# Placing side work by TensorE time: half of the next image's preparation moved, and a step put between an operation and its transposes

## The chip, the cores and the metric

The kernel runs on one core of a Trainium2 chip. The metric is the device time of one execution in microseconds; the kernel before takes 1912.11 us, the median of three runs. Five engines work side by side on the core, each through its own list of instructions: TensorE (PE, matmuls and transposes), VectorE (DVE), ScalarE (ACT), GpSimd (POOL) and SyncE (SP), which here issues the transfers.

## The reference

The input is four images of 32 channels by 128 x 128 points, in float32. Two layers follow each other.

```python
# layer 0: attention over the 4096 positions of an image
xs = x.reshape(B, C, h, R, w, R).transpose(0, 1, 3, 5, 2, 4).reshape(B, C*R*R, h, w)   # R = 2
q = xs.reshape(B, C*R*R, 4096)                       # 128 values of 4096 positions
energy = einsum('bci,bcj->bij', q, q)
energy = energy / (d[:, :, None] * d[:, None, :])
attn = softmax(energy, axis=-1)
out = gamma * einsum('bcj,bij->bci', q, attn) + xs
# layer 1: on 4096 tokens of 128 values per image as the kernel lays them out
t = t + attn_linear(layer_norm(t))     # K, Q, V with 8 heads, K^T V first, no softmax
t = t + moe(layer_norm(t))             # 8 experts, the best two of a softmax router
```

In the kernel an image of layer 0 is a matrix of 4096 positions by 128 values. Its scaled energies are symmetric, so the kernel computes only one half of them and uses each block twice. Layer 1 works on 32 groups of 128 tokens by 128 values. It uses that K^T V is a product with the Gram matrix of the normalised tokens, so that one Gram matrix of 128 x 128 stands for all tokens.

## The kernel before

**Layer 0, `attend(b)`.** The 4096 positions are cut into 8 chunks of 512, and a chunk into 4 blocks of 128. The outer loop runs over the chunk `i`, the inner over the chunks `jc` up to and including `i`, and then over the 4 blocks `j` of `jc`. One step is: a matmul of 512 columns for the energies (`pe`, L272), the exponential on ScalarE (`pr`, L274), and a matmul that adds this block to the output of chunk `i` (`po`, L240). For `jc < i`, VectorE also transposes the exponentials in squares of 32 (`F`, L281), 16 transfers put the squares into place (`G`, L295), and four matmuls (`pg`, L209) add the other half to the output of chunk `jc`, followed by a VectorE addition (`o`, L219). These four come `LAG` units later than the block they belong to, from the list `late`. The blocks on the diagonal are shorter, and need transposes of their own (`ptd`, L251). An image has 144 steps.

**The preparation, `prep(b, kc)`.** A quarter of an image (two chunks) is loaded (`xx`), turned on TensorE (`ptq`, L173), copied by VectorE into `qT` (L176), squared and summed (`sq`, `ss`, L184 and L185), sent to GpSimd for the power of minus one half (`rn`, L111), multiplied by it (`qs`, L192), turned again on TensorE (`ptn`, L195) and copied by ScalarE into `qn` (L197), which the energies read. It is a generator with 9 steps.

**Layer 1, `layer1(b, st, alone)`.** A generator of about 166 steps. Its first half divides the outputs of layer 0 by the sums (`pbd` transposes on TensorE, `df` on VectorE, the addition into `T` on GpSimd), takes row statistics (`bs`, then a power on GpSimd), normalises on ScalarE (`xn`, L366) and adds up the Gram matrix (`pgram`, L409). Its second half applies the attention (`pat`, L464), normalises again (`xg`, L366), turns the result (`ptf`, L483), routes (`route`), turns the gates (`ptg`, L552), and runs the eight experts (`py`, L566 and L573).

**What sets the order.** The generators are side work: the loop at the end of the kernel draws steps from them between the steps of `attend`, so that their small operations lie between large matmuls. Each stream has a first step, a last step and a count, and the position is the number of the attention step:

```python
        else:
            streams.append((work_left, BEGIN, 140, SIDE))
        if b + 1 < B:
            for kc, at in enumerate((96, 124, 131, 137)):
                streams.append((prep(b + 1, kc, states[b + 1]), at, at + 9, 9))
```

So layer 1 of image `b - 1` runs inside the attention of image `b`, from step 14 to step 140, and all four quarters of image `b + 1` are prepared in the last third of image `b`. Layer 1 of the last image runs alone at the end (`alone` is true). What the loop draws is a wish: when the program is built, the framework may still move an instruction on its engine when it judges that its operands come late, but on the chip each engine takes its list in order. Buffers come from pools: `qn` has 11 buffers (`npool`), `qT` 5, the PSUM tiles `pt` and `py` two each, `po` and `pg` one each.

Of the kernel before, what the change touches and what calls it, by code (L numbers as in the profile page):

```python
# [10 lines left out]
F32 = mybir.dt.float32  # L11
# [8 lines left out]
def kernel(  # L20
# [35 lines left out]
    nc = tc.nc  # L56
    P = 128
# [4 lines left out]
    NCH = N // CH  # L62
    NJ = CH // P
    HW2 = W // 2
    KT = 32
# [4 lines left out]
    const = ctx.enter_context(tc.tile_pool(name="const", bufs=1))  # L70
    xin = ctx.enter_context(tc.tile_pool(name="xin", bufs=2))
    qpool = ctx.enter_context(tc.tile_pool(name="qpool", bufs=5))
    npool = ctx.enter_context(tc.tile_pool(name="npool", bufs=11))
    big1 = ctx.enter_context(tc.tile_pool(name="big1", bufs=1))
    opool = ctx.enter_context(tc.tile_pool(name="opool", bufs=NCH + 2))
    ppool = ctx.enter_context(tc.tile_pool(name="ppool", bufs=6))
# [2 lines left out]
    work = ctx.enter_context(tc.tile_pool(name="work", bufs=2))  # L79
# [7 lines left out]
    def psum_t(name):  # L87
        return ps_t.tile([P, CH], F32, tag="pt", name=name)
# [14 lines left out]
    ebd = const.tile([P, 4, D], F32, tag="eb", name="ebd")  # L103
# [6 lines left out]
    def pow_neg_half(dst, src):  # L110
        nc.gpsimd.tensor_tensor(dst, src, neg_half.to_broadcast(list(src.shape)), ALU.pow)  # L111
# [37 lines left out]
    def tokens(ap, b):  # L149
        return ap[b].rearrange("c (s k r) w -> s r c k w", s=2, r=2)  # L150
# [9 lines left out]
    def prep(b, kc, st):  # L160

        xx = xin.tile([P, 8, HW2, 2], F32, tag="xx", name=f"xx_{b}_{kc}")
        load_tokens(xx.rearrange("p k w r -> p k (w r)"), b, 8 * kc, 8)
        qT = qpool.tile([P, 2, NJ, P], F32, tag="qT", name=f"qT_{b}_{kc}")
        st.setdefault("qT", {})[2 * kc] = qT[:, 0]
        st["qT"][2 * kc + 1] = qT[:, 1]
        yield
        for g in range(2):
            pt = psum_t(f"ptq_{b}_{kc}_{g}")
            for jj in range(2):  # L170
                for r2 in range(2):
                    k = 4 * g + 2 * jj
                    nc.tensor.transpose(  # L173
                        pt[:, ts(2 * jj + r2, P)], xx[:, k : k + 2, :, r2].rearrange("p k w -> p (k w)"), ident
                    )
            nc.vector.tensor_copy(  # L176
                qT[:, :, 2 * g : 2 * g + 2, :].rearrange("p s j (r c) -> p (j r) s c", c=64),
                pt.rearrange("p (m s c) -> p m s c", s=2, c=64),
            )
            yield  # L180
        ss = stat.tile([P, 2 * NJ], F32, tag="ss", name=f"ss_{b}_{kc}")
        for s in range(2):
            sq = work.tile([P, NJ, P], F32, tag="sq", name=f"sq_{b}_{kc}_{s}", bufs=1)
            nc.vector.tensor_tensor(sq, qT[:, s], qT[:, s], ALU.mult)  # L184
            nc.vector.tensor_reduce(ss[:, ts(s, NJ)], sq, AX.X, ALU.add)  # L185
            yield
        rn = stat.tile([P, 2 * NJ, 1], F32, tag="rn", name=f"rn_{b}_{kc}")
        pow_neg_half(rn[:, :, 0], ss)
        yield
        for s in range(2):  # L190
            qs = work.tile([P, NJ, P], F32, tag="qs", name=f"qs_{b}_{kc}_{s}", bufs=2)
            nc.vector.tensor_tensor(qs, qT[:, s], rn[:, ts(s, NJ)].to_broadcast([P, NJ, P]), ALU.mult)  # L192
            pt = psum_t(f"ptn_{b}_{kc}_{s}")
            for j in range(NJ):
                nc.tensor.transpose(pt[:, ts(j, P)], qs[:, j, :], ident)  # L195
            qn = npool.tile([P, CH], F32, tag="qn", name=f"qn_{b}_{2 * kc + s}")
            nc.scalar.activation(qn, pt, AF.Copy)  # L197
            st.setdefault("qn", {})[2 * kc + s] = qn
            yield

    late = []
    clock = [0]
# [110 lines left out]
    def layer1(b, st, alone):  # L313
# [166 lines left out]
        def expert_rows(g):  # L480
            pt = psum_s(f"ptf_{b}_{g}")
            for j in range(4):
                nc.tensor.transpose(pt[:, ts(j, P)], normed[g][:, j, :], ident)  # L483
            nc.scalar.activation(xn[:, ts(g, 4), :], pt.rearrange("p (j t) -> p j t", t=P), AF.Copy)
# [42 lines left out]
            yield  # L527

        for u in range(6):
            for g in (2 * u, 2 * u + 1):  # L530
                if u < 4 and not alone:
                    transpose_rows(g)
                    yield
            if 0 <= u - 1 < 4:
                la = yield from attention_rows(u - 1)
                yield from row_stats(f"f{b}", u - 1, rsf, nbf)
                yield
                router_rows(u - 1, la)
                yield
            for g in (2 * u - 4, 2 * u - 3):  # L540
                if 0 <= u - 2 < 4:
                    norm_rows(g)
                    expert_rows(g)
                    yield
            if u in (2, 4):
                yield from route(u // 2 - 1)


        dst = tokens(out, b)
        for g in range(KT // 4):  # L550
            pt = psum_s(f"ptg_{b}_{g}")
            nc.tensor.transpose(pt[:, :P], gate[:, 4 * g : 4 * g + 16, :].rearrange("p j e -> p (j e)"), ident)  # L552
            gT = work.tile([P, P], F32, tag="gT", name=f"gT_{b}_{g}", bufs=2)
            nc.vector.tensor_copy(gT, pt[:, :P])
            pb = psum_s(f"pbe_{b}_{g}")
            nc.tensor.matmul(pb, gT, ebd.rearrange("p j c -> p (j c)"), start=True, stop=True)  # L556
            acc = work.tile([P, 4, D], F32, tag="acc", name=f"acc_{b}_{g}", bufs=2)
            nc.vector.tensor_tensor(acc, T[:, ts(g, 4), :], pb.rearrange("p (j c) -> p j c", c=D), ALU.add)
            yield
            for jj in range(2):  # L560
                tmp = work.tile([P, 2, 4, D], F32, tag="wide", name=f"tmp_{b}_{g}_{jj}")
                for jk in range(2):
                    j = 2 * jj + jk
                    k = 4 * g + j
                    py = psum_y(f"py_{b}_{k}_0")
                    nc.tensor.matmul(py, xn[:, k, :], ew_sb[:, 0:4, :], start=True, stop=True)  # L566
                    for e in range(4):
                        nc.vector.scalar_tensor_tensor(  # L568
                            acc[:, j, :], py[:, ts(e, D)], gate[:, k, e : e + 1], acc[:, j, :], ALU.mult, ALU.add
                        )  # L570
                    yield
                    py = psum_y(f"py_{b}_{k}_1")
                    nc.tensor.matmul(py, xn[:, k, :], ew_sb[:, 4:8, :], start=True, stop=True)  # L573
                    for e in range(4):
                        nc.scalar.activation(  # L575
                            tmp[:, jk, e, :], py[:, ts(e, D)], AF.Copy, scale=gate[:, k, 4 + e : 5 + e]
                        )
                    yield
                nc.gpsimd.tensor_tensor(tmp[:, :, 0:2], tmp[:, :, 0:2], tmp[:, :, 2:4], ALU.add)  # L579
                nc.gpsimd.tensor_tensor(tmp[:, :, 0], tmp[:, :, 0], tmp[:, :, 1], ALU.add)  # L580
                rows = acc[:, 2 * jj : 2 * jj + 2, :]
                nc.gpsimd.tensor_tensor(rows, rows, tmp[:, :, 0], ALU.add)
            for s in range(2):
                for r1 in range(2):
                    p0 = s * 64 + r1 * 32
                    nc.sync.dma_start(dst[s, r1, :, ts(g, 4), :], acc[p0 : p0 + 32])


    states = [{} for _ in range(B)]
    STEPS = NJ * NCH * (NCH + 1) // 2  # L590
    LAST = STEPS - NJ * NCH
    SIDE = 166
    BEGIN = 14

    first = prep(0, 0, states[0])
    next(first)
    load_weights()
    for _ in first:
        pass

    for b in range(B):
        streams = []
        if b == 0:
            for kc, begin, end in ((1, 0, 8), (2, 10, 26), (3, 30, 60)):
                streams.append((prep(0, kc, states[0]), begin, end, 9))
            streams.append((setup_weights(), 60, 70, 3))
        else:
            p = states[b - 1]
            work_left = layer1(b - 1, p, False)
            streams.append((work_left, BEGIN, 140, SIDE))  # L610
        if b + 1 < B:
            for kc, at in enumerate((96, 124, 131, 137)):
                streams.append((prep(b + 1, kc, states[b + 1]), at, at + 9, 9))
        done = [0] * len(streams)
        for t, _ in enumerate(attend(b, states[b])):
            for n, (steps, begin, end, count) in enumerate(streams):
                while t >= begin and done[n] * (end - begin) < (t + 1 - begin) * count:
                    next(steps, None)
                    done[n] += 1
        for steps, *_ in streams:  # L620
            for _ in steps:
                pass
# [42 lines left out]
```

## Time and profile before

| | before |
|---|---|
| three runs, us | 1914.57, 1911.74, 1912.11 |
| span of the profiled execution, us | 1915.9 |
| TensorE busy, share of the span | 95% |
| VectorE, ScalarE, GpSimd busy | 47%, 51%, 15% |
| granted TensorE clock, mean | 0.978 |
| share of TensorE on the chain that ended last | 79% |

A profile of one execution has several views. The page gives the busy time of each engine and the granted TensorE clock by slice. The view of waits says who waited for whom, with the total, the number and the longest, in microseconds. The view of windows gives, for a stretch of time, its length, the busy time with the number of records, the granted clock, the share of the transfer engines and their rate. The timeline lists instructions in order of time, with the idle time before them in brackets. A name on the left of an arrow is written, the names on the right are read.

### The profile page before, as it was taken

How to read it: one execution, taken by the hardware profiler on the slowest of the kernel's cores; microseconds unless marked ns; L12 is line 12 of the kernel's file. 1: busy time of each engine (PE TensorE's matmuls, PEld its weight loads, DVE VectorE, ACT ScalarE, POOL GpSimd, SP SyncE). 2: the span in 40 equal slices, each digit the busy share in tenths (PEclk: the TensorE clock that was granted, in tenths of full speed). 3: DMA queues.
4: the chain of work that ended last, by engine and by line, in shares of the span. 5: the costliest groups of instructions: out<-in, count | busy, mean ns of one | idle time of the engine just before them, and what ended most of it. 6: DMA issues, size and time to landing. Idle time of an engine off the chain costs nothing.

```text
span 1915.9 us, 21142 instructions
## 1 busy us (share of the span) xinstructions
PE 1817.3 (95%) x5474; PEld 921.4 (48%) x5474; DVE 907.9 (47%) x2201; ACT 974.8 (51%) x3117; POOL 293.1 (15%) x279
## 2 busy tenths in 40 slices
PE   6999999988999999999999999999999999999588
PEld 4445444444554444445555444445555544444543
DVE  3333232435355454543555445453545544543676
ACT  2554445445456555444657555444465654554454
POOL 0000000003000222201200122210210022220336
PEclk9999999999999999999999999999999999999789
DMA  5333334322232232343232323233422233245001
GB/s 117 77 87 75 95 90 106 95 69 61 66 86 69 58 90 73 78 110 76 56 83 71 88 65 85 70 84 76 99 64 67 72 74 77 73 97 117 1 11 34
DMA packets 142247, 145.68 MB, mean 76 GB/s; under 512 B 32528, under 2 KB 84784, under 8 KB 142128
## 3 DMA queue, kind: packets, MB, share of 16 engines
q1 hardware_dynamic: 138496, 142.73, 31.0%
q10 hardware_dynamic: 3632, 1.60, 0.4%
q8 instruction: 45, 0.74, 0.2%
q14 instruction: 74, 0.61, 0.1%
HBM read 18.38 MB, written 8.39 MB: 14 GB/s over the span
## 4 chain that ended last, share of the span: by engine, by line
PE 79%; DVE 8%; SPq 4%; POOL 4%; ACT 2%; DMA 2%; issue 1%; ACTq 0%; DVEq 0%; POOLq 0%
PE po L240 22%; PE pe L272 19%; PE pg L209 17%; PE py L573 5%; PE py L566 5%; SPq L295 4%; PE pat L464 1%; PE pbe L556 1%; DVE F L281 1%; DVE df L383 1%; POOL rsa L111 1%; PE ptd L251 1%; PE ptn L195 1%; DVE bs_a L352 1%; PE pgram L409 1%
## 5 line engine op out<-in xcount | busy, mean ns | idle before, releaser
L274 ACT ACTIVATE pr<-pe 128x512 f32<-128x512 f32 (+1 forms) x576 | 323.7, 562 | 526.7 <-PE pe L272 523.3
L240 PE MATMUL po<-pr,qT 128*128 128x512 f32 (+3 forms) x1152 | 551.9, 561 | 9.3 <-ACT pr L274 7.6
L281 DVE STREAM_TRANSPOSE F<-pr 128x512 f32<-128x512 f32 x448 | 311.5, 705 | 387.0 <-ACT pr L274 349.1
L272 PE MATMUL pe<-qn,qn 128*128 128x512 f32 x896 | 459.4, 594 | 0.0
L209 PE MATMUL pg<-G,qT 128*128 128x512 f32 x896 | 443.8, 597 | 7.6 <-DVE o L219 7.4
L240 PEld LDWEIGHTS po<-pr,qT 128*128 128x128 f32 x1152 | 213.6, 191 | 239.9 <-issue 188.2
L214 ACT ACTIVATE junk<-G 128x512 bf16<-128x512 f32 x448 | 276.7, 625 | 2.6 <-DMA G<-F 2.1
L209 PEld LDWEIGHTS pg<-G,qT 128*128 128x128 f32 x896 | 167.9, 192 | 203.8 <-issue 184.3
L575 ACT ACTIVATE tmp<-py,gate 128x128 f32<-128x128 f32 x512 | 145.3, 371 | 179.1 <-PE py L573 168.7
L272 PEld LDWEIGHTS pe<-qn,qn 128*128 128x128 f32 x896 | 159.2, 191 | 145.5 <-issue 145.4
L568 DVE SCALAR_TENSOR_TENSOR acc<-py,gate,acc 128x128 f32<-128x128 f32 x512 | 175.1, 348 | 107.9 <-PE py L566 95.3
L219 DVE TENSOR_TENSOR o<-o,pg 128x512 f32<-128x512 f32 x112 | 76.6, 684 | 195.0 <-PE pg L209 193.9
L579 POOL TENSOR_TENSOR tmp<-tmp 128x512 f32<-128x512 f32 x64 | 81.4, 1272 | 511.4 <-ACT tmp L575 511.3
L573 PE MATMUL py<-ew_sb,xn 128*128 128x512 f32 x256 | 132.8, 605 | 3.8 <-ACT tmp L575 3.8
L566 PE MATMUL py<-ew_sb,xn 128*128 128x512 f32 x256 | 130.1, 595 | 0.0
L274 ACT ACTIVATION_READ_ACCUMULATOR pr<-pe 128x1 f32 x576 | 115.1, 200 | 0.0
L111 POOL TENSOR_TENSOR rn<-ss,neg_half 128x8 f32<-128x8 f32 x16 | 26.2, 1640 | 501.8 <-DVE ss L185 501.8
L272 PE MATMUL pe<-qn 128*128 128x512 f32 (+3 forms) x256 | 90.1, 442 | 0.0
L214 ACT ACTIVATION_READ_ACCUMULATOR junk<-G 128x1 f32 x448 | 88.5, 197 | 0.0
L573 PEld LDWEIGHTS py<-ew_sb,xn 128*128 128x128 f32 x256 | 48.7, 194 | 64.2 <-issue 53.0
L111 POOL TENSOR_TENSOR rsf<-dm_f,neg_half 128x8 f32<-128x8 f32 x16 | 26.3, 1642 | 339.7 <-DVE dm_f L361 339.7
L566 PEld LDWEIGHTS py<-ew_sb,xn 128*128 128x128 f32 x256 | 48.0, 191 | 58.3 <-issue 43.0
(121 smaller groups left out, 1441.3 us busy)
## 6 DMA issues: line engine op xcount, KB each, us to landing
G<-F SPq DMA_DIRECT2D x1792, 64.0 KB, 2.0
xx<-in_x_dram SPq DMA_DIRECT2D x64, 128.0 KB, 2.9
T<-in_x_dram SPq DMA_DIRECT2D x16, 512.0 KB, 7.2
out_dram<-acc SPq DMA_DIRECT2D x128, 64.0 KB, 1.8
ew_sb<-in_L_ffn_expert_w_dram ACTq DMA_DIRECT2D x1, 512.0 KB, 5.4
raw_w<-in_L_attn_Wv_dram ACTq DMA_DIRECT2D x1, 512.0 KB
raw_w<-in_L_attn_Wk_dram ACTq DMA_DIRECT2D x1, 256.0 KB
raw_w<-in_L_attn_Wq_dram ACTq DMA_DIRECT2D x1, 256.0 KB
```

The costliest lines, as they stand in the source:

```text
L209: nc.tensor.matmul(pg.rearrange("p (a f) -> p a f", a=4), st["qT"][i][:, ib, :], G[:, :, ib], start=(ib == 0), stop=(ib == NJ - 1),)
L214: nc.scalar.activation(junk, G[:, :, ib], AF.Copy, accum_out=st["sums"][:, NJ * i + ib, jc : jc + 1])
L240: nc.tensor.matmul(po[:, lo:hi], qT[blk // NJ][:, blk % NJ, :], w, start=(count[0] == 1), stop=(count[0] == total))
L272: nc.tensor.matmul(pe[:, c0:], qn[jc][:, ts(j, P)], qn[i][:, c0:], start=True, stop=True)
L274: nc.scalar.activation(pr[:, c0:], pe[:, c0:], AF.Exp, accum_out=sums[:, t, i : i + 1])
L281: nc.vector.transpose(Fb[:, :, :, j, :], pr)
L295: nc.sync.dma_start(G[ts(q, S), a].rearrange("p ib f -> p (ib f)"), F[ts(a, S), q].rearrange("p ib j c -> p (ib j c)"),)
L566: nc.tensor.matmul(py, xn[:, k, :], ew_sb[:, 0:4, :], start=True, stop=True)
L568: nc.vector.scalar_tensor_tensor(acc[:, j, :], py[:, ts(e, D)], gate[:, k, e : e + 1], acc[:, j, :], ALU.mult, ALU.add)
L573: nc.tensor.matmul(py, xn[:, k, :], ew_sb[:, 4:8, :], start=True, stop=True)
L575: nc.scalar.activation(tmp[:, jk, e, :], py[:, ts(e, D)], AF.Copy, scale=gate[:, k, 4 + e : 5 + e])
L579: nc.gpsimd.tensor_tensor(tmp[:, :, 0:2], tmp[:, :, 0:2], tmp[:, :, 2:4], ALU.add)
```

## The change

Four things change. The side work is placed by `clock`, which counts the TensorE work of the attention in units, as a percentage of the image's `UNITS`, and no longer by the number of the step; layer 1 gets 7% to 97%. Quarters 2 and 3 of the next image are prepared inside that image (2% to 20% and 30% to 50%), quarters 0 and 1 still in the image before (66% to 84% and 85% to 99%); the pool of `qn` then has 10 buffers. In `prep` the two multiplications become steps of their own, before the transposes that need them, and the count of steps is 10. In `layer1` the second half is reordered: the attention rows of a group come before the next group's `ptx` transposes, the `ptf` transposes of a group come one step after its normalisation, and the gates are turned ahead of the group that uses them. It is meant to give each chain of VectorE, GpSimd and ScalarE operations some TensorE work to hide behind.

```diff
-    npool = ctx.enter_context(tc.tile_pool(name="npool", bufs=11))
+    npool = ctx.enter_context(tc.tile_pool(name="npool", bufs=10))
...
+        scaled = []
         for s in range(2):
             qs = work.tile([P, NJ, P], F32, tag="qs", name=f"qs_{b}_{kc}_{s}", bufs=2)
             nc.vector.tensor_tensor(qs, qT[:, s], rn[:, ts(s, NJ)].to_broadcast([P, NJ, P]), ALU.mult)
+            scaled.append(qs)
+            yield
+        for s, qs in enumerate(scaled):
             pt = psum_t(f"ptn_{b}_{kc}_{s}")
...
         for u in range(6):
+            if 0 <= u - 1 < 4:
+                la = yield from attention_rows(u - 1)
             for g in (2 * u, 2 * u + 1):
                 if u < 4 and not alone:
                     transpose_rows(g)
                     yield
             if 0 <= u - 1 < 4:
-                la = yield from attention_rows(u - 1)
                 yield from row_stats(f"f{b}", u - 1, rsf, nbf)
...
             for g in (2 * u - 4, 2 * u - 3):
-                if 0 <= u - 2 < 4:
+                if 0 <= g - 1:
+                    expert_rows(g - 1)
+                    yield
+                if 0 <= g:
                     norm_rows(g)
-                    expert_rows(g)
                     yield
             if u in (2, 4):
                 yield from route(u // 2 - 1)
+        expert_rows(KT // 4 - 1)
+        yield
...
-        for g in range(KT // 4):
+        gates = {}
+
+        def transpose_gate(g):
             pt = psum_s(f"ptg_{b}_{g}")
...
+        transpose_gate(0)
+        yield
+        for g in range(KT // 4):
...
+                if jj == 0 and g + 1 < KT // 4:
+                    transpose_gate(g + 1)
...
-            streams.append((work_left, BEGIN, 140, SIDE))
+            streams.append((layer1(b - 1, states[b - 1], False), 7, 97, 161))
         if b + 1 < B:
-            for kc, at in enumerate((96, 124, 131, 137)):
-                streams.append((prep(b + 1, kc, states[b + 1]), at, at + 9, 9))
+            nxt = states[b + 1]
+            streams.append((prep(b + 1, 0, nxt), 66, 84, 10))
+            streams.append((prep(b + 1, 1, nxt), 85, 99, 10))
+            carried.append((prep(b + 1, 2, nxt), 2, 20, 10))
+            carried.append((prep(b + 1, 3, nxt), 30, 50, 10))
         done = [0] * len(streams)
-        for t, _ in enumerate(attend(b, states[b])):
+        start = clock[0]
+        for _ in attend(b, states[b]):
+            t = 100 * (clock[0] - start) / UNITS
             for n, (steps, begin, end, count) in enumerate(streams):
-                while t >= begin and done[n] * (end - begin) < (t + 1 - begin) * count:
+                while t >= begin and done[n] * (end - begin) < (t - begin) * count:
```

## The prediction

> **What bounds the kernel now.** I read the page first (engines, slices, clock), then the waits of TensorE, then windows cut at the stages, then a timeline of the longest wait.
>
> ```profile
> PE 1817.3 (95%) x5474; PEld 921.4 (48%) x5474; DVE 907.9 (47%) x2201; ACT 974.8 (51%) x3117; POOL 293.1 (15%) x279
> PE   6999999988999999999999999999999999999588
> PEclk9999999999999999999999999999999999999789
> ```
>
> TensorE is busy from slice 1 to slice 36; no other engine comes near. So the time is TensorE's work plus what TensorE loses. What it loses has names:
>
> ```profile
> PE ptn L195 <- DVE qs L192: 26.1, 8, 6.4
> ...
> PE po L240 <- ACT pr L274: 7.6, 6, 2.6
> ...
> PE pg L209 <- DVE o L219: 7.4, 6, 1.9
> PE ptf L483 <- ACT xg L366: 5.9, 6, 3.0
> ```
>
> The first line is the preparation: its second transposes wait for the scaled rows. Where these losses lie, the windows tell (time, busy, records, clock, transfer share, rate). I take as lost in a window its length minus busy times clock, so that a slow clock counts too.
>
> ```profile
> 341.00:364.00 23.00, 20.04 (x56) 0.93 0.32 80
> 364.00:386.00 22.00, 20.63 (x63) 1.00 0.43 108
> 386.00:408.00 22.00, 15.45 (x58) 0.84 0.33 79
> 440.00:490.00 50.00, 43.07 (x164) 0.97 0.28 70
> 550.00:796.00 246.00, 246.00 (x684) 1.00 0.31 76
> 796.00:816.00 20.00, 18.09 (x45) 0.91 0.31 76
> 837.00:866.00 29.00, 25.10 (x82) 0.88 0.43 105
> 899.00:930.00 31.00, 27.95 (x100) 0.94 0.35 81
> 1757.00:1810.00 53.00, 35.63 (x184) 0.81 0.22 43
> ```
>
> Between the stages nothing is lost (550 to 796: 246.00 of 246.00 at full clock). Lost are 22 - 15.45 x 0.84 = 9.0 us in 386 to 408, and in the same way 4.4, 1.4, 8.2, 3.5, 6.9 and 4.7 us in the other short ones. Images 2 and 3 repeat each other: the windows 1257:1277, 1298:1327 and 1360:1391 again lose 3.5, 6.9 and 4.7. The first 30 us lose 16.4; the last 159 us (layer 1 of the last image, alone) lose 24.1 + 18.8 + 11.5 = 54.4. The sum over all windows is some 132 us, of which about 59 lie between head and tail. Only those 59 are within reach of most of the change.
>
> The longest wait in the timeline:
>
> ```profile
> 389.04 1.11 PE L173 MATMUL ptq<-ident,xx 128*128 128x128 f32 x8
> ...
> 394.03 1.64 POOL L111 TENSOR_TENSOR rn<-ss,neg_half 128x8 f32<-128x8 f32 x1 [21.72 <-DVE ss L185]
> 395.70 1.29 DVE L192 TENSOR_TENSOR qs<-qT,rn 128x512 f32<-128x512 f32 x2 [1.81 <-POOL rn L111]
> ...
> 396.54 1.94 PE L195 MATMUL ptn<-ident,qs 128*128 128x128 f32 x8 [6.39 <-DVE qs L192]
> ```
>
> From the first transposes to the second the chain takes 396.54 - 389.04 = 7.5 us: two copies, four squares and sums of 0.69 us each, the power of 1.64, one multiplication. The eight transposes of `ptq` cover 1.1 us of it, and nothing else lies between.
>
> **What the Trainium skill says.** "TensorE: Matmul & The Clock Gate", What's actually happening: after an idle window of about 3.4 us the array runs at half clock until it was busy as long again. The trace agrees in kind: the window with the 6.39 us wait shows 0.84, the stretch of 246 us without a wait 1.00. So a long wait costs more than its length: 386 to 408 lost 9.0 us for waits of 6.6. "PSUM — Partial Sum Buffer", Engine vs sequencer instructions: ScalarE and VectorE queues are strictly in order, and matmuls start in program order. The trace agrees: at 445 us `po` waits 2.49 us for an exponential that stood behind eight `xn` of the side work on ScalarE (3.18 us). "Perfetto Trace Analysis", Optimization Strategy: find the gaps of the engine that binds, see what it waits for, and make that start sooner. That is the change.
>
> **The change, part by part.** No matmul, copy or transfer is added or removed; only order and buffers change. I read the order of each engine's list in both built programs, and count the TensorE work between two places by durations of the trace: 0.86 us for a 512-column matmul (two records, start to start), 0.11 us for a 128-column transpose.
>
> *Quarters 2 and 3 leave the image's end.* In images 1, 2 and 3 some 43 to 44 us of TensorE work now lie between the last `ptq` and the first `ptn` of these quarters, where 5.1 us (quarter 2) and 0.0 (quarter 3) lay at the first boundary, and 2.6 for quarter 3 at the others. The chain of 7.5 us is hidden. The windows that held them lost 1.4 + 9.0 + 6.9 + 6.9 = 24.2. What stays: the short diagonal steps at the start of an image now stand without filling, and there `po` follows its exponential closely; the start of the first image, where they stand almost alone too, shows waits of 0.54 (`ptn`) and 0.30 (`po`) right after the head. I take 1.5 us for each of three images, and 1 us once because `pg_7_5` and `pg_7_6` stand back to back in image 1 (the one place of before with that order waited 0.78). 24.2 - 4.5 - 1.0 = 17.7 us saved.
>
> *Quarters 0 and 1 stay.* For image 1, the list has 4.7 us between `ptq` and `ptn` of quarter 0 (before 5.1) and 3.5 for quarter 1 (before 3.4). The waits of 1.24 and 2.96 stay; +0.4. The two extra steps do nothing there, since the built order puts the transposes as near as before. For images 2 and 3 the gap grows from 12 to 41 us, but no wait on `qs` was left there. What was lost there (3.5 each) is VectorE standing at `qs` for GpSimd's power, so that `o` (L219) came late and `pg` waited 1.91 us. In the new list of VectorE `qs` of quarter 1 still follows its sums by one `acc`, so this may recur; I save half, 3.5 in all.
>
> *Layer 1, first half.* Lost: 8.2 + 4.7 + 4.7 = 17.6. Here ScalarE's `xn` waits for the chain over GpSimd and holds up the exponentials. In the new list the four Gram groups of image 2 stand at 49, 73, 81 and 85 us of the image's TensorE work, before at 61, 63, 72 and 80, so the chain has more room; but `pr` still stands behind eight `xn`, and quarter 2's eight VectorE operations of 0.69 to 0.77 us and one power precede the denominators. Nothing saved is the one bound, 14 us the other (0.5% of 160 us stays in any case as the gaps between matmuls); I take a third, 6.
>
> *Layer 1, second half.* The `ptf` transposes waited 0.51 us once per image with 0.6 us of slow clock; now another group lies between. The windows 490:550, 960:1010 and 1421:1471 lost 1.55 each, half of it on `pg`. Saved: 0.7 x 3 = 2. The gates' earlier turn hides behind `py` matmuls in both.
>
> *The tail.* VectorE's and GpSimd's lists are the same until the gates. The first `ptf` now stands behind three more matmul groups, but it waited 3.92 us for the row statistics, which don't move; ScalarE's list is nearly the same. `py` of a group's second half changes its PSUM pool with the gate's turn; at 0.86 us each, two matmuls (1.7 us) lie between use and reuse of a bank, against 1.1 to 1.4 us for ScalarE's four reads. I take 0, bounds -5 and +5. Head: `ptn` of quarter 1 stands later, 0.5 saved. The pool of 10 holds 8 chunks and the 2 of the one quarter prepared early; quarter 1 comes when the first two are free, so no wait.
>
> Sum: 17.7 - 0.4 + 3.5 + 6 + 2 + 0.5 = 29.3. 1912.1 - 29.3 = 1882.8; I say 1883.
>
> **The rivals.**
> *The first half of layer 1 opens up.* If the spread lets `xn` come in time everywhere and the `pg` waits vanish too, 14 instead of 6 and 7 instead of 3.5: 1912 - 29 - 8 - 3.5 = 1871. For it: the wider spacing. Against: ScalarE's order.
> *The waits move.* The start of each image loses as much as its end did (3 us more per image), the first half saves nothing: 1883 + 9 + 6 = 1898. For it: the chain den, `rd`, `pbd` now stands right behind `qs` on VectorE in images 2 and 3. Against: 12 us of TensorE work lie there.
> *Slower.* If the two moved quarters hold up the critical chains of layer 1 on VectorE and GpSimd, each could cost its 7.5 us plus some 1.7 us of slow clock: three images x 2 x 9.2 = 55 against 27 saved otherwise: about 1940. For it: VectorE is in order, and a `qs` waiting on the power blocks the queue. Against: VectorE is at 47%, and layer 1 has 45 us around these steps.
>
> **How the numbers follow.** Forecast 0.55; layer 1 opens up 0.20; waits move 0.18; slower 0.05; 0.02 for no difference (1908 to 1916). Range 1866 to 1902: the first rivals with the tail's 5 us below and 4 above. Faster 0.93, same 0.02, slower 0.05.
>
> **What would show it.** Right: the line of `ptn` falls from 26.1 to about 10.5 us (6.3 in the head, 1.2 and 3.0 before image 1); the clock at the boundaries to images 2 and 3 is 0.97 or more; the tail still lasts some 159 us. Wrong: new waits of `pbd`, `pgram` or `po` in the first 100 us of an image, a tail that differs by over 5 us, or `ptn` waiting inside an image.

## The result, and the profile after

| | before | changed |
|---|---|---|
| median, us | 1912.67 (1911.74 to 1914.57, 4 runs) | 1888.45 (1888.02 to 1892.35, 4 runs) |
| ratio, 95% interval | | 0.9877 (0.986 to 0.9894) |
| span of the profiled execution, us | 1915.9 | 1886.6 |

The change makes the kernel 24 us faster: 1.23%, with an interval from 1.06 to 1.40%. The page of the changed kernel, the same rows as before:

```profile
PE 1799.0 (95%) x5474; PEld 915.4 (49%) x5474; DVE 909.5 (48%) x2201; ACT 974.6 (52%) x3117; POOL 293.7 (16%) x279
...
PE   6999999998999999999999999999899999999678
...
PEclk9999999999999999999999999999999999999789
```

TensorE still bounds the time. Its row had two 8s side by side, at the boundary to image 1 and just behind it (383 to 479 us); it now has one at 424 to 471 us, and one inside image 3 that is new (1320 to 1368 us). Both now lie in layer 1's first half. The waits of TensorE of the changed kernel (total, times, longest, us):

```profile
PE po L244 <- ACT pr L278: 11.6, 11, 1.9
PE ptq L173 <- DMA xx<-in_x_dram: 9.6, 1, 9.6
PE ptn L199 <- DVE qs L193: 9.2, 2, 6.3
PE ptd L255 <- ACT gd L257: 9.0, 3, 5.1
...
PE pg L213 <- DVE o L223: 1.6, 2, 0.8
```

`ptn` fell from 26.1 us in 8 waits to 9.2 in 2 (the head, and one of 2.96 before image 1), and `pg` from 7.4 to 1.6. In exchange `po` waits 11.6 us for exponentials (7.6 before), and `ptd` 9.0 us for `gd` (1.1 before). The windows at the boundaries and in layer 1's first half of the changed kernel (time, length, busy, clock, transfers):

```profile
358.00:402.00 44.00, 38.79 (x123) 0.96 0.39 90
780.00:800.00 20.00, 19.67 (x47) 1.00 0.33 80
821.00:850.00 29.00, 28.81 (x98) 1.00 0.53 120
1232.00:1252.00 20.00, 19.67 (x47) 1.00 0.34 82
1273.00:1302.00 29.00, 28.81 (x98) 1.00 0.54 122
...
415.00:494.00 79.00, 74.26 (x283) 0.98 0.30 75
864.00:946.00 82.00, 76.67 (x287) 0.94 0.27 65
1317.00:1398.00 81.00, 73.98 (x284) 0.96 0.27 66
```

The boundaries to images 2 and 3 are clean: 28.81 of 29.00 at full clock. The first half of layer 1 is not: 82 - 76.67 x 0.94 = 9.9 us are lost in image 2, with the clock at 0.94.

The clock of a window of 80 us comes in steps of 0.02, so a loss worked out so is good to about 1 us. For the comparison of kernels I use a finer account: at a mark, the start of that matmul in the trace, minus the durations of all that stands ahead of it in TensorE's list (0.427 us for 512 columns in one record, 0.107 for a transpose). What this difference grows by between two marks was lost between them. How large a row is depends a little on the durations taken for the smallest matmuls; the differences between kernels do not, since all have the same matmuls. The marks are the first energies of an image, its first `pbd`, the first energies of chunk 4 and those of chunk 7. Losses in us, for the two kernels and for three that are told below:

| stretch | before | changed | move alone | all early | addition on VectorE |
|---|---|---|---|---|---|
| head, and image 0 up to chunk 7 | 29.0 | 25.6 | 29.3 | 25.3 | 25.9 |
| boundary to image 1 (chunk 7 to the first `pbd`) | 18.7 | 14.0 | 11.9 | 24.0 | 14.1 |
| boundaries to images 2 and 3 | 26.0 | 6.4 | 11.8 | 8.4 | 6.4 |
| layer 1, first half, three images (to chunk 4) | 27.9 | 29.6 | 24.1 | 27.9 | 14.3 |
| three images, chunk 4 to chunk 7 | 13.9 | 11.3 | 13.1 | 7.3 | 11.3 |
| last image from chunk 7, and the tail | 49.0 | 48.2 | 47.7 | 48.2 | 46.3 |
| sum | 164.5 | 135.1 | 137.9 | 141.1 | 118.3 |

The sums differ by 29.4 for before and changed, and the spans of the two profiled executions by 1915.9 - 1886.6 = 29.3.

### The profile page after: what moved, and what is told of

Read it like the earlier page. It is cut to its first block, busy times and chain, and to the rows that moved or that the text cites. A ratio compares the mean times of both kernels' runs of the same rounds, so it can differ in the third digit from the quotient of the medians.

```text
span 1886.6 us, 21105 instructions
## 1 busy us (share of the span) xinstructions
PE 1799.0 (95%) x5474; PEld 915.4 (49%) x5474; DVE 909.5 (48%) x2201; ACT 974.6 (52%) x3117; POOL 293.7 (16%) x279
## 3 DMA queue, kind: packets, MB, share of 16 engines
q1 hardware_dynamic: 138496, 142.73, 31.5%
## 4 chain that ended last, share of the span: by engine, by line
PE 81%; DVE 7%; SPq 4%; POOL 3%; ACT 2%; DMA 1%; issue 1%; ACTq 0%; POOLq 0%; DVEq 0%
PE po L244 23%; PE pe L276 20%; PE pg L213 18%; PE py L588 5%; PE py L581 5%; SPq L299 4%; PE pbe L571 1%; PE pat L468 1%; PE pgram L413 1%; DVE F L285 1%; PE ptd L255 1%; POOL rsa L111 1%; DVE df L387 1%; POOL T L395 1%; PE ptn L199 1%
## 5 line engine op out<-in xcount | busy, mean ns | idle before, releaser
L244 PE MATMUL po<-pr,qT 128*128 128x512 f32 (+3 forms) x1152 | 551.1, 561 | 16.4 <-ACT pr L278 11.6
L583 DVE SCALAR_TENSOR_TENSOR acc<-py,gate,acc 128x128 f32<-128x128 f32 x512 | 177.7, 349 | 118.3 <-PE py L581 104.6
L370 ACT ACTIVATE xn<-T,nba,rsa 128x128 f32<-128x128 f32 x128 | 51.9, 481 | 55.1 <-DVE nba L367 55.1
L588 PEld LDWEIGHTS py<-ew_sb,xn 128*128 128x128 f32 x256 | 48.5, 191 | 61.9 <-issue 53.0
```

The lines of the kernel that those rows point to most:

```text
L244: nc.tensor.matmul(po[:, lo:hi], qT[blk // NJ][:, blk % NJ, :], w, start=(count[0] == 1), stop=(count[0] == total))
L583: nc.vector.scalar_tensor_tensor(acc[:, j, :], py[:, ts(e, D)], gate[:, k, e : e + 1], acc[:, j, :], ALU.mult, ALU.add)
```

## The experiments

All ratios are to the kernel before, with a 95% interval. Of the changed kernel it is 0.9877 (0.986 to 0.9894), so a ratio within some 0.002 of it isn't told from it.

### Which part cleared the boundaries

**The move alone**, put into the kernel before:

```diff
...
-            for kc, at in enumerate((96, 124, 131, 137)):
+            for kc, at in enumerate((96, 124)):
                 streams.append((prep(b + 1, kc, states[b + 1]), at, at + 9, 9))
+            carried.append((prep(b + 1, 2, states[b + 1]), 4, 34, 9))
+            carried.append((prep(b + 1, 3, states[b + 1]), 44, 76, 9))
```

> The kernel before with one part of the change alone: quarters 2 and 3 prepared inside the image that uses them, by step number; everything else (step numbers, layer 1's order, no extra step) as before. Theory (the move is worth its 17.6 us by itself, the rest 7): about 1894 us, 0.9905 of before. Rival (it needs the placement by TensorE time, since steps at the start of an image are short): above 1900 us, with new waits of ptn, pbd or pgram in the first 100 us of images 1 to 3.

Measured: 1891.75 us, ratio 0.9882 (0.9865 to 0.9898). That is nearly all of the change. The waits of `ptn` fall to 11.0 us, with no new one of `ptn` or `pbd` in the images; those of `pgram` rise from 12.7 us in 4 waits to 19.2 in 6, and the first half of layer 1 doesn't suffer from it (24.1 us, 27.9 before).

**All quarters early**, in the changed kernel, with 11 buffers for `qn` as before:

```diff
...
-            streams.append((prep(b + 1, 1, nxt), 85, 99, 10))
-            carried.append((prep(b + 1, 2, nxt), 2, 20, 10))
-            carried.append((prep(b + 1, 3, nxt), 30, 50, 10))
+            streams.append((prep(b + 1, 1, nxt), 84, 90, 10))
+            streams.append((prep(b + 1, 2, nxt), 90, 95, 10))
+            streams.append((prep(b + 1, 3, nxt), 94, 99, 10))
```

> The changed kernel, but quarters 2 and 3 of the next image are prepared at the end of the image before again (by the TensorE clock: 84 to 90, 90 to 95 and 94 to 99 per cent for quarters 1, 2, 3), with 11 buffers for the scaled chunks. Theory (the move of the two quarters is what saves, 17.6 us of the 24 to 29): about 1905 us, some 17 above the changed kernel, and the waits of ptn on qs come back to 20 us or more, at the boundaries. Rival (the placement by TensorE time is what saves, wherever the quarters lie): 1888 to 1892 us, ptn below 12 us.

Measured: 1894.39 us, ratio 0.9893 (0.9878 to 0.9908). My theory was wrong by 10 us, though the waits of `ptn` did come back to 21.5 us as it said: 6.3 of them are in the head as in every kernel, 12.7 before and at the start of image 1, 1.25 each at images 2 and 3. Windows of this kernel, first the boundary to image 1, then that to image 2:

```profile
374.00:427.00 53.00, 42.94 (x143) 0.90 0.25 60
...
846.00:878.00 32.00, 31.87 (x104) 1.00 0.55 110
```

At the start of image 1 it loses 53 - 42.94 x 0.90 = 14.4 us, at the start of image 2 next to nothing, though all four quarters stand at the image's end again. The waits of `ptn` say the same (timeline of this kernel):

```profile
382.94 1.91 PE L199 MATMUL ptn<-ident,qs 128*128 128x128 f32 x8 [4.24 <-DVE qs L193]
...
396.89 1.94 PE L199 MATMUL ptn<-ident,qs 128*128 128x128 f32 x8 [5.53 <-DVE qs L193]
...
843.23 1.23 PE L199 MATMUL ptn<-ident,qs 128*128 128x128 f32 x8 [1.25 <-DVE qs L193]
```

So the move and the rest of the change are two remedies for one loss. At the boundaries to images 2 and 3 the account has 26.0 us before, 11.8 with the move alone, 8.4 with the rest without the move, 6.4 with both. Only at image 1 is the move needed (24.0 without it, 14.0 with it). The rest holds the placement of the quarters by TensorE time, the steps between `qs` and its transposes, and the edits of layer 1. Which of them does it without the move was not tested one by one; the placement is the likeliest, since in the runs below, with the move in place, each of the others is worth at most some 5 us there.

**Three quarters early**: quarter 1 at 84 to 91%, quarter 2 at 91 to 99%, only quarter 3 inside the image; `qn` has 11 buffers.

```diff
...
-            streams.append((prep(b + 1, 1, nxt), 85, 99, 10))
-            carried.append((prep(b + 1, 2, nxt), 2, 20, 10))
+            streams.append((prep(b + 1, 1, nxt), 84, 91, 10))
+            streams.append((prep(b + 1, 2, nxt), 91, 99, 10))
```

> The changed kernel, but quarter 2 too is prepared in the image before (84 to 91 and 91 to 99 per cent for quarters 1 and 2), and only quarter 3 stays inside the image. Theory (ScalarE's order costs the first half of layer 1 its 10 us): the first half keeps its loss within 2 us per image, and the boundaries lose about 3 us each again: about 1897 us. Rival (quarter 2's operations in the image's first fifth cost it): the first half loses 3 us less per image, which pays for the boundaries: 1886 to 1890 us.

Measured: 1894.3 us, ratio 0.9893 (0.9878 to 0.9908), between what the theory and the rival said, and the same as with all quarters early. The account has 30.3 us for layer 1's first half (29.6 in the changed kernel): taking quarter 2 out of the image's first fifth frees nothing there, so its operations aren't the cause of that loss. The boundary to image 1 costs 3 us more.

### The smaller parts

**No extra step** (`qs` and its four transposes in one step again; the count of steps is 9).

```diff
...
-            scaled.append(qs)
-            yield
-        for s, qs in enumerate(scaled):
...
```

> The changed kernel without the extra step: the scaling of a half and its four transposes stand in one step again. Theory (the transposes' place in the list is set by the placement, not by the step): 1888 us, within 3. Rival (the step is what spares pg and ptn their waits in images 2 and 3): 6 us more, about 1894, with waits of ptn on qs inside the images.

Measured: 1891.85 us, ratio 0.9885 (0.9869 to 0.9901): not told from the changed kernel. The account shows two differences that nearly cancel: the boundaries to images 2 and 3 lose 11.7 instead of 6.4 us (among them `py`, 2.17 us for an `acc` that stands behind other work on VectorE), and layer 1's first half 25.6 instead of 29.6.

**The old order of layer 1's second half.**

```diff
-            if 0 <= u - 1 < 4:
-                la = yield from attention_rows(u - 1)
             for g in (2 * u, 2 * u + 1):
                 if u < 4 and not alone:
                     transpose_rows(g)
                     yield
             if 0 <= u - 1 < 4:
+                la = yield from attention_rows(u - 1)
...
-                if 0 <= g - 1:
-                    expert_rows(g - 1)
-                    yield
-                if 0 <= g:
+                if 0 <= u - 2 < 4:
                     norm_rows(g)
+                    expert_rows(g)
...
```

> The changed kernel with the order of layer 1's second half as before (norm and expert rows of one group in one step, attention after the transposes, the gate transposed right ahead of its use). Theory (worth 0.8 us in each of three images, nothing in the tail): 2.5 us more, about 1891, with ptf waiting on xg again some 0.5 us per image and a tail from the last image's end that is the same within 1 us. Rival (the reorder matters in the tail, where layer 1 is alone): 5 us or more, about 1894 or above, all of it in the last 150 us.

Measured: 1884.59 us, ratio 0.9846 (0.9832 to 0.9861): faster than the changed kernel, where both theories had it slower. The gain lies where nothing was edited: the first half of layer 1 loses 24.6 us instead of 29.6. All of it is in images 2 and 3; in image 1, ahead of which no second half of layer 1 stands, the first half loses the same. The tail loses 1 us more. One thing comes with this edit: inside an image the generator of layer 1 has 160 steps in the changed kernel and 151 in the old order (in the kernel before too, where the text ahead says about 166), while the count stays at 161, so layer 1 also ends some 5% of an image earlier. The run doesn't tell the two apart.

**Layer 1 placed by step number** (14 to 140), the preparation by TensorE time.

```diff
-            streams.append((layer1(b - 1, states[b - 1], False), 7, 97, 161))
+            streams.append((layer1(b - 1, states[b - 1], False), 14, 140, 161))
...
-            t = 100 * (clock[0] - start) / UNITS
             for n, (steps, begin, end, count) in enumerate(streams):
+                t = number if count == 161 else 100 * (clock[0] - start) / UNITS
```

> The changed kernel with layer 1 placed by step number (14 to 140) as before, the preparation still by TensorE time. Theory (in the first half placement by time gave nothing, it lost 2 us per image there): the first half loses about 2 us less per image and the others stay: 1882 to 1889 us. Rival (placement by time is what keeps layer 1 spread, and without it the waits of before come back): 1893 us or more.

Measured: 1884.76 us, ratio 0.9843 (0.9828 to 0.9858). As the theory said: 24.2 us in the first half, and 3.4 us more at the boundaries to images 2 and 3.

**Both of the last two together.** The edit is the sum of the two above.

> The changed kernel with two of its parts undone together: layer 1 placed by step number (14 to 140), and its second half in the order of before. What is left is the move of the two quarters, the placement of the preparation by TensorE time and the extra step. If the two parts cost independently (3.7 and 3.9 us seen one at a time by the medians): about 1881 us. If they cost through the same place (the built order of ScalarE in layer 1's first half): 1884 us, no better than either alone.

Measured: 1893.53 us, ratio 0.9899 (0.9884 to 0.9914). Neither theory: the first half loses 23.6 us, no less than with either alone, and from chunk 4 to chunk 7 17.1 us are lost instead of 11.3, with a new wait of the gates (waits of TensorE of this kernel):

```profile
PE pbe L560 <- DVE gT L558: 5.0, 3, 2.4
```

The gates' late turn by itself doesn't bring this wait: the kernel before turns them late and runs layer 1 by step number too, and its `pbe` waits 0.2 us in all. What in this list brings it stays open.

### What the first half of layer 1 waits for

The new `ptd` wait of the changed kernel, in its timeline:

```profile
886.39 2.35 POOL L395 TENSOR_TENSOR T<-T,df 128x1024 f32<-128x1024 f32 x1 [1.70 <-DVE df L387]
...
888.77 0.87 DVE L356 BATCH_NORM_STATS2 bs_a<-T 128x6 f32<-128x128 f32 x4 [2.46 <-POOL T L395]
...
890.87 2.47 DVE L285 STREAM_TRANSPOSE F<-pr 128x512 f32<-128x512 f32 x4
...
894.50 1.64 POOL L111 TENSOR_TENSOR rsa<-dm_a,neg_half 128x8 f32<-128x8 f32 x1 [5.76 <-DVE dm_a L365]
...
896.38 2.80 ACT L370 ACTIVATE xn<-T,nba,rsa 128x128 f32<-128x128 f32 x7 [3.89 <-DVE nba L367]
...
900.33 0.47 PE L255 MATMUL ptd<-ident,pr 128*128 128x128 f32 x1 [3.45 <-ACT gd L257]
```

A group of eight rows goes from the start of the addition on GpSimd (886.39) to that of `nba` (896.17) in 9.8 us, twice over GpSimd: 2.35 us for the addition, 1.64 for the power. Between the two, VectorE also works off other things of its list, the four `F` among them. ScalarE stands 3.89 us at the group's first `xn`, and with it the exponential and the `gd` behind it. This leaves three suspects: that `xn` comes in blocks on ScalarE, that it stands on ScalarE at all, and that the chain is late.

**`xn` one round later** inside an image:

```diff
-        for kc in range(6):
+        lag = 0 if alone else 1
+        for kc in range(6 + lag):
...
-                for k in range(8 * kc - 8, 8 * kc):
+            if 1 + lag <= kc < 5 + lag:
+                for k in range(8 * (kc - lag) - 8, 8 * (kc - lag)):
```

> The changed kernel, but within an image the normalisation of a group of eight rows on ScalarE (and its Gram products) comes one round later than its statistics. Theory (the first half of layer 1 loses about 10 us per image because eight xn in a row stand on ScalarE ahead of the exponentials and wait there for the chain over GpSimd): these waits of po and pgram fall, the first half loses 3 to 6 us less per image, 1873 to 1880 us. Rival (the loss comes from quarter 2's operations on VectorE and GpSimd in the same stretch): no gain, 1887 to 1890 us.

Measured: 1890.57 us, ratio 0.9875 (0.986 to 0.989): no gain. `po` waits 21.2 us for exponentials in 18 waits, the longest 3.7.

**A step after every two normalisations** inside an image (177 steps instead of 161):

```diff
                     normalise(xn[:, k, :], k, rsa, nba)
+                    if k % 2 and not alone:
+                        yield
...
```

> The changed kernel with a step after every two normalisations of layer 1's first half, so that exponentials stand between them on ScalarE. Theory (eight xn in a row hold up the exponentials): the waits of po on pr fall by half, first half 2 to 4 us less per image: 1876 to 1882 us. Rival (the xn wait for nba, and the exponentials behind them with them, however they are grouped): 1886 to 1890 us.

Measured: 1883.67 us, ratio 0.9838 (0.9823 to 0.9852). Faster than the changed kernel, but not for the reason I gave. The waits of `po` grow to 18.7 us, and the account gains at the boundaries (16.4 us in all instead of 20.4) and from chunk 4 on (10.0 instead of 11.3), while the first half loses 30.6. Its longest wait, in its timeline:

```profile
896.58 0.49 ACT L370 ACTIVATE xn<-T,nba,rsa 128x128 f32<-128x128 f32 x1 [3.84 <-DVE nba L367]
...
897.70 1.50 PE L244 MATMUL po<-pr,qT 128*128 128x512 f32 x2 [3.19 <-ACT pr L278]
```

One single `xn` ahead of the exponential is enough: it waits as long for `nba` as seven did. So the block isn't what costs this wait.

**`xn` on VectorE** inside an image:

```diff
-                    normalise(xn[:, k, :], k, rsa, nba)
+                    if alone:
+                        normalise(xn[:, k, :], k, rsa, nba)
+                    else:
+                        nc.vector.tensor_scalar(
+                            xn[:, k, :], T[:, k, :], rsa[:, k, :], nba[:, k, :], ALU.mult, ALU.add
+                        )
```

> The changed kernel, but inside an image the normalisation of layer 1's first half runs on VectorE (behind nba in the same list) and not on ScalarE; the last image's layer 1, which is alone, keeps ScalarE. Theory (the exponentials stand behind xn on ScalarE, and xn behind the chain over GpSimd): the waits of po on pr and of ptd on gd go to under 4 us in all, images 2 and 3 lose 4 to 5 us less each in their first half: 1876 to 1880 us. Rival (the 8 x 0.28 us more per group on VectorE delay its transposes F and the divisions df as much): 1886 to 1894 us, with waits of pbd or pg on VectorE.

Measured: 1891.12 us, ratio 0.9884 (0.9868 to 0.9901). The rival holds. The waits for ScalarE do fall (`po` on `pr` from 11.6 to 5.5 us), and the first half loses 31.5 us. Its timeline in image 2:

```profile
889.16 2.34 POOL L395 TENSOR_TENSOR T<-T,df 128x1024 f32<-128x1024 f32 x1 [5.32 <-DVE df L387]
...
889.33 2.26 DVE L500 TENSOR_TENSOR lw<-nba,srw 128x64 f32<-128x64 f32 x1
...
891.99 0.69 DVE L308 COPY o<-po 128x512 f32<-128x512 f32 x1
...
892.82 1.87 PE L244 MATMUL po<-pr,qT 128*128 128x512 f32 x2 [3.62 <-DVE dm_a L364]
```

`po` has one PSUM bank, and the profile names `dm_a`, which ran beside the end of the copy `o` that frees it (892.68). Now that copy is late, because VectorE stands still while GpSimd adds: `lw`, an operation of 0.21 us elsewhere, takes 2.26, until the addition ends at 891.50. A wait of 3.6 us has gone from one queue to the other.

**The addition on VectorE**, in every image:

```diff
-                    nc.gpsimd.tensor_tensor(tk, tk, df.rearrange("p k w r -> p k (w r)"), ALU.add)
+                    nc.vector.tensor_tensor(tk, tk, df.rearrange("p k w r -> p k (w r)"), ALU.add)
```

> The changed kernel with the residual addition (T plus df, 128x1024, 2.35 us on GpSimd) on VectorE, estimated at 1.4 us from twice the 0.69 us of a 128x512 operation there; in every image. Theory (whatever stands in order behind a group's chain df, T, statistics, power, nba waits, because the chain itself is late; the queue only decides who shows the wait): the chain is about 1.2 us shorter per group and VectorE no longer idles 2.5 us for T, so the first half of layer 1 loses 1 to 2 us less per image, the tail 2 to 4 us less: 1879 to 1884 us. Rival (only the order of the queues counts; 1.4 us more on VectorE per group delays its transposes F): 1887 us or more, with the same wait of 2.5 to 3.7 us per image.

Measured: 1871.24 us (1870.52 to 1871.7), ratio 0.9777 (0.9763 to 0.9791), 17 us faster than the changed kernel and beyond what the theory gave. The addition takes 1.20 us on VectorE (2.35 on GpSimd). In the account nothing moves by more than 0.3 us except the first half (14.3 instead of 29.6) and the tail (46.3 instead of 48.2). The same stretches in windows:

```profile
415.00:491.00 76.00, 72.51 (x285) 1.00 0.31 78
861.00:937.00 76.00, 73.77 (x288) 1.00 0.29 71
1308.00:1383.00 75.00, 73.12 (x282) 1.00 0.29 71
```

The clock is back at 1.00. In the changed kernel, TensorE had half clock for 3.4 us at 445, 3.4 at 885, 6.8 at 899 and 6.8 at 1350 us; here it has none between 371 and 1732 us. TensorE's waits of over 0.25 us in the three first halves fall from 17.0 us to 7.6, the longest from 5.15 to 1.70. The chain of image 2 in this kernel's timeline:

```profile
881.80 1.21 DVE L395 TENSOR_TENSOR T<-T,df 128x1024 f32<-128x1024 f32 x1
...
890.38 1.64 POOL L111 TENSOR_TENSOR rsa<-dm_a,neg_half 128x8 f32<-128x8 f32 x1 [4.10 <-DVE dm_a L365]
...
892.25 0.49 ACT L370 ACTIVATE xn<-T,nba,rsa 128x128 f32<-128x128 f32 x1 [0.94 <-DVE nba L367]
...
893.90 0.33 PE L255 MATMUL ptd<-ident,pr 128*128 128x128 f32 x1 [0.75 <-ACT gd L257]
```

ScalarE stands 0.94 us instead of 3.89, and `ptd` 0.75 instead of 3.45. Counted from the image's first `pbd`, this `nba` comes only some 1 us earlier (31 against 32 us), and from the start of the addition to it the chain is no shorter: 10.3 us against 9.8. What did change is that the built list has two `xn` ahead of `gd` here and eight in the changed kernel, and that VectorE's statistics no longer wait for GpSimd's addition (12.1 us in 9 waits in the changed kernel, 3.3 in 3 before, none here). This run therefore shows that the addition's place on GpSimd brings half of the loss, 15 of 29.6 us, but not by which of these ways.

**Addition on VectorE and the split** of the normalisations:

> The changed kernel with both edits that helped most: the residual addition on VectorE, and a step after every two normalisations in layer 1's first half. If the late chain was the whole of the first half's loss, the split adds only what it gave outside it (about 1 us per image at the boundaries and at pe_5): 1866 to 1870 us. If the split took its gain from the same wait: 1871 to 1874 us, no better than the addition alone.

Measured: 1874.06 us, ratio 0.9799 (0.9786 to 0.9812). Not better than the addition alone: the split gains 2.2 us at the boundary to image 1, 2.0 at the others and 1.2 after chunk 4, as it did before, but the first half loses 20.1 us instead of 14.3, and the tail 2.4 more. The addition alone stays the best version.

## Why the prediction was right, and where it was not

**What bounds, and what the change is worth.** 1883 was predicted and 1888.5 measured, inside the range. The working has a slip: 24.2 - 4.5 - 1.0 is 18.7 and not 17.7, so its terms add to 30.3 and the forecast should have been 1882. That this lies near the 29.3 us between the two profiled executions is luck. Layer 1's first half was put 7.7 us too high and the boundaries with the moved quarters 0.6; the boundaries to images 2 and 3 ahead of the image's start were put 3.1 too low, the head 2.9, the tail 0.8 and the second half 0.6.

The base was wrong besides: the losses were read in an execution of 1917.65 us, and I subtracted them from the median of 1912.1. From the right base the forecast is 1917.65 - 30.3 = 1887.4. Executions of the kernel before lay between 1910.3 and 1917.9 us in all the runs. Those above 1914 us with a clock on record show a mean of 0.978 to 0.979, with one exception, and those below 1912.3 one of 0.981 or 0.982; by an estimate, 0.003 of 1817 us of busy TensorE is 5.5 us, which would cover the 5 us of the profiled one. In which stretches they lie stays open.

**Quarters 2 and 3 leave the image's end: size right in sum, reason half right.** 18.7 us by the terms. In the stretches that held them (chunk 7 of image 0 to the first `pbd` of image 1; the start to the first `pbd` of images 2 and 3) the account saves 4.7 + 6.5 + 6.5 = 17.7. By image it is less even: the terms gave 7.9 for image 1 and 5.4 for each of the others. What I took for the cause, the move, is enough by itself (the move alone) but is needed only at image 1. At images 2 and 3 the rest of the change clears the boundary without it (all early). I had not asked whether two edits remove the same loss.

**Quarters 0 and 1 stay: right at image 1, too small at the others.** The waits of 6.3 and 2.96 us stayed as said; the one of 1.24 fell to 0.75, so `ptn` waits 9.2 us for `qs` and not 10.5. For images 2 and 3, 3.5 us were predicted and 6.6 saved (from chunk 7 to the next image): the waits of `pg` fell from 7.4 to 1.6 us, not by half. The step "the two extra steps do nothing there" is too strong; without them these stretches and the image starts lose 5.3 us more.

**Layer 1, first half: the step that failed.** 6 us were to be saved, and 1.7 more were lost; the bounds of 0 and 14 don't hold it. In image 1 the account saves 2.6 us: `po` waited 2.5 and 2.6 us for exponentials there, and now waits 1.2 and 1.1, with a new wait of 2.1 for a copy. In images 2 and 3 it loses 2.5 and 1.8 us more: `ptd` now waits 3.45 and 5.15 us for `gd` (0.6 before), and the clock falls with it. I argued from the places of the Gram groups that "the chain has more room". The chain did end earlier for three of the four groups of image 2 (`nba` at 16, 21, 32 and 50 us after the image's first `pbd`; before at 31, 35, 43 and 47). That saved nothing there: `gd`, which `ptd` needs, stands behind `xn` in ScalarE's list, and ScalarE stood 9.0 us at the first `xn` of three groups of image 2, before 4.4 us at two. Changing the order only changed who waits, on ScalarE (the split, the lag) or on VectorE (`xn` on VectorE). With the addition off GpSimd 15 of the 29.6 us go; by which way stays open. Quarter 2's operations, which I had also named, are not it (three early).

The same stretch is at the mercy of the list that is built. Edits elsewhere in the source moved it from 29.6 to 25.6 (no extra step) and 24.6 (old second half), and from 27.9 to 24.1 (move alone). This is the likely reason why two parts of the change, tested by undoing them, look harmful by 0.3% each and aren't when both are undone. Whether either part is harmful in itself stays open.

**Layer 1, second half; tail; head.** 2 us predicted, 2.6 saved from chunk 4 to 7. Tail 0 predicted, 0.8 saved, and it lasts as long as before. The head with image 0: 0.5 predicted, 3.4 saved. The move alone, which leaves image 0 placed by step number, saves nothing there (29.3 against 29.0), so it is most likely the placement of image 0's own quarters and of `setup_weights`, which I had not counted; no run tests it alone.

**The rivals.** "The waits move" was named for its cause at the image's start, which didn't come; but its second half, no saving in the first half of layer 1, did. So did one of the prediction's own signs of being wrong: `po` waits 1.9 us for exponentials some 50 us after the start of images 2 and 3. "Slower" did not come: the moved quarters held up nothing.

## What to carry to other kernels

Take the base of a forecast from the same execution as its losses. Before adding the gains of several edits, ask whether two of them remove the same wait, and test each alone as well as undone: here the move alone gave 1.18% and the rest without the move 1.07%, together 1.23%. Where a wait moves from one engine's queue to another's whenever the order is changed, try what its operands come from instead: one addition moved from GpSimd to VectorE gave 17 us by the medians, where edits of the order gave at most 5.

## What the hardware showed beside this

While GpSimd runs an addition, some operations of VectorE stand still until it ends. The Trainium skill says in "GPSIMD Engine Reference", 1. Specifications, that the SBUF interfaces are shared with VectorE, with contention for VectorE instructions with two SBUF inputs or in a two-port mode; how long they are held, that section does not say. The traces agree, and show the length. In the kernel before, `dm_a` (128x8, two inputs from SBUF, 0.16 us elsewhere) took 2.35 us at 927.52, starting 0.04 us after an addition on GpSimd of 2.37; `qs` (0.69 us elsewhere) took 1.75 us at 800.48 beside two GpSimd operations of 1.27 and 1.06. The stream transposes (`F`), which have one input, were not stretched: in the changed kernel five of them lie wholly inside an addition into `T`, and took 0.69 to 0.71 us, as elsewhere.

Over all operations of VectorE that took at least 0.15 us more than their median beside GpSimd, this adds up to 9.0 us of VectorE time in the changed kernel and 5.6 with the addition on VectorE. Only one of them lies in a first half of layer 1 of the changed kernel (`sv_a` at 426.56, 1.60 us instead of 0.17). So it can be only a small part of the 15 us gained there.
